# A 14-unit wait in the order planner of a four-layer gated cross-attention kernel: group 1 joins the last attention later

## The chip, the core and the metric

The kernel runs on one core of a Trainium2 chip. The metric is device time in microseconds (us) of one execution; lower is better. A core has one matmul engine (TensorE, PE in the profile; its weight loads are listed as PEld), a vector engine (DVE), an activation engine (ACT), a general-purpose engine (POOL) and an engine that here only issues DMA transfers (SP). Each works through its own instruction list strictly in the order in which the program wrote it; they meet through semaphores.

## What is computed

The input is `x` of 4 batches of 256 tokens with 128 features, and a context of the same size. Four layers follow one another; each adds a gated cross-attention and then a gated feed-forward to `x`. What matters here is the end of layer 2 and layer 3:

```python
x = x + tanh(g_xattn[2]) * L2_xattn(layernorm(x), ctx, ctx)      # 16 heads of 8
x = x + tanh(g_ffn[2])   * L2_ffn(layernorm(x), ...)             # quantised matrix + LoRA
x = x + tanh(g_xattn[3]) * L3_xattn(layernorm(x), ctx, ...)      # 16 heads of 64
x = x + tanh(g_ffn[3])   * L3_ffn(layernorm(x), ...)             # 8 experts, best 2 per token

def L3_xattn(latents, context, ...):
    q  = layernorm(latents) @ Wq;  k, v = split(layernorm(context) @ Wkv)
    a  = softmax(clip(q k^T / 8, -11, 11))
    return (a v) @ Wo + bo

def L3_ffn(x, ...):
    top2 of softmax(x @ gate_w^T)                  # two experts for each token
    y  = sum over the two of w_e * (silu(x @ gate_e) * (x @ up_e)) @ down_e
    return y + (silu(x @ sh_gate) * (x @ sh_up)) @ sh_down
```

All arithmetic is in 32-bit floats.

## The kernel before

**Groups and streams.** The four batches form two groups of two: group 0 holds batches 0 and 1, group 1 holds batches 2 and 3. `chain(g)` (L1370) takes one group through all layers. The kernel does not leave the order of the instructions to a scheduler: `tc.manual_schedule` (L1395) keeps on all five engines the order in which Python issued them. That order comes from a small planner (L240 to L256). A `Stream` is a Python generator which issues some instructions and then yields a number, its own estimate of how long they take. `run_streams` always advances the stream whose planned time `at` is lowest, and adds the yielded number to it. So a yielded number is a position in the plan and no instruction: nothing in the finished program waits for it. Group 1 starts `LATER` = 28 units behind group 0, and the second batch of a group `BETWEEN` = 16 units behind its first.

**Layer 2 and the join.** `attention8` (L306) computes layer 2's attention for one batch, `finish2` (L1190) its feed-forward. For each batch of the group one such stream is made (`second`, L1389). `attention64` (L569) then runs layer 3's attention of the two batches as one software pipeline, and its `begin(h)` joins the layer-2 stream of a batch before it starts that batch (`start3`, L1227).

**Layer 3's attention.** For each batch there are four steps. The tiles carry names such as `sc_a3_1_2` (layer 3, batch 1, chunk 2); the texts below write `sc_1_2` for short. Per step PE does: `pw_qh`, `pw_kh` (projections, L444), `sc` (two score tiles, L472), `pv` (values, L458), `po` (weighted values, L486), `ps` (row sums, L501). ACT takes the exponential of the scores (L1214) and DVE clips it (L1215). Then `divide` (L517): DVE takes the reciprocal of the row sums (`rs`, L518, 128x256) and, for the second batch of a group, PE spreads it over the rows (`pb`, L526) and DVE multiplies (L533); for the first batch it goes by DMA through memory (L538, L543) to L550. `output` (L553) makes `pf_a` and adds to `x` (L567). `start3` needs two layernorms of `x` and one of the context, each transposed on PE (`pt_lT`, `pt_cT`, L1221).

**Routing and experts.** `prepare3` (L1239) makes for each batch the layernorm `x3f`, its transposition (`pt_f`, L294), the router's logits (`f3lg`, L1248) and their softmax, whose exponential runs on ACT (L644). `route3` (L1288) needs both batches of the group: on DVE it finds the best two experts of each token (`hot_f`, L686), on PE it counts tokens for each expert (`pc_f`, L691), on DVE it computes each token's slot (`si_f`, L725), and POOL scatters the rows (`rows_f`, eight indirect DMAs, L744). Beside it `shared3` (L1257) computes the shared expert (`pp_f3sh`, `sl_f3sh`, `f3hs`, `py_f3s`). `feed3` (L1310) fetches the sorted rows (`xs_f`, L770) and runs 15 blocks of 128 slots. A block takes from DVE a copy of the expert's weights (`st_f`, L808) and of the rows (`xT_f`, L1318), from PE a transposition (`pt_f`, L810), eight matmuls (`pp_f`, L1324) and four of the block before (`py_f`, L819), from ACT the activation (`sl_f`, L1283), and from DVE the product (`h_f`, L1284). The down weights of a block come by DMA (`wd_f`, L801). At the end come a store (L826), eight gathers on POOL (L851), sums on DVE and the store of `x`.

**Buffers and tables.** PSUM gives eight tiles of one bank in turn to all of these. ACT's exponential and its activation of the experts lie in different tables, so a change from one to the other inserts a table load, which some of the lines below show as `ACT_TABLE_LOAD`.

The functions that the diff touches, and what calls them:

Of the kernel before, what the change touches and what calls it, by code (L numbers as in the profile page):

```python
# [21 lines left out]
G = 2  # L22
# [6 lines left out]
FEATS, PAIRS, VALUES = 20, 7, 5  # L29
BLOCK = P  # L30
LATER = 28.0
BETWEEN = 16.0
ROUND = 12582912.0

# [2 lines left out]
def flamingo_kernel(ctx: ExitStack, tc: tile.TileContext, a: dict, out: bass.AP):  # L37
# [52 lines left out]
    def load(name, shape, src, tag=None):  # L90
        t = wts.tile(shape, F32, tag=tag or name, name=name, bufs=1)
        nc.sync.dma_start(out=t, in_=src)
        return t

    def expert_weights(name, width, src):

        t = wts.tile([P, E, 1024], F32, tag="wexp", name=name, bufs=1)
        for e in range(E):
            nc.sync.dma_start(out=t[:, e, 0:width], in_=src[e])
        return t  # L100
# [157 lines left out]
    def joined(*others):  # L258
        while not all(s.done for s in others):
            yield 0.5  # L260
# [308 lines left out]
    def attention64(batches, start, done, after):  # L569

        hs = [Heads64(b) for b in batches]
        begun, ends = {}, []
        for h, before in zip(hs, [None] + hs):
            h.before = before
        steps = [(h, cp) for h in hs for cp in range(4)]

        def at(n):
            return steps[n] if 0 <= n < len(steps) else None  # L580

        def begin(h):
            yield from joined(after[h.b])
            yield from start(h)

        def ended(h):
            yield HOP
            yield from h.divide()
            yield from h.output()
            yield HOP  # L590
            yield from done(h.b)

        for n in range(-2, len(steps)):
            if n == -2 or (n % 4 == 0 and n // 4 + 1 < len(hs)):
                h = hs[0 if n == -2 else n // 4 + 1]
                begun[h] = Stream(begin(h))
            two, one, this = at(n + 2), at(n + 1), at(n)
            if two and two[1] == 0:
                yield from joined(begun[two[0]])
            if one:  # L600
                one[0].scores(2 * one[1])
                yield 0.9
            if two:
                two[0].project(two[1])
                yield 1.7
            if this:
                this[0].values(this[1])
                yield 1.3
                this[0].sums(this[1])
                yield 0.9  # L610
                if this[1] == 3:
                    ends.append(Stream(ended(this[0])))
            if one:
                one[0].scores(2 * one[1] + 1)
                yield 0.9
            if one and one[1] % 2 == 0:
                one[0].project_values(one[1] // 2)
                yield 1.7
            if two and two[1] == 3:
                two[0].projected = True  # L620
        yield from joined(*ends)
# [453 lines left out]
    def route1(g):  # L1075
        fe, ne, scs, again = zip(*(normed1[G * g + i] for i in range(G)))
        sc = small.tile([P, GT, E], F32, tag="lg", name=f"f1s_{g}")
        for i in range(G):
            nc.vector.tensor_copy(sc[:, i * T : (i + 1) * T, :], scs[i])
        m = small.tile([P, GT], F32, tag="smm", name=f"f1m_{g}")  # L1080
        nc.vector.tensor_reduce(m, sc, AX.X, ALU.max)
        hot = yield from first_is_max(sc, m, f"f1_{g}")
        yield 0.5
        r = Routed(g, f"f1_{g}")
        yield from r.assign([hot], lambda t: ne[t // T][0][:, t % T, :], again)

        al = small.tile([P, GT], F32, tag="al", name=f"f1al_{g}")
        nc.scalar.activation(al, m, AF.Sigmoid)
        pw = ps_mm([E, GN], f"f1pw_{g}")
        for t in range(GT):  # L1090
            nc.tensor.matmul(pw[:, t * P : (t + 1) * P], lhsT=hot[:, t, :], rhs=ident, start=True, stop=True)
        hotT = feat(f"f1hT_{g}")[0:E, :]
        evac(hotT, pw)
        yield 1.5
        pb = ps_mm([P, GT, D], f"f1pb_{g}")
        for t in range(GT):
            nc.tensor.matmul(pb[:, t, :], lhsT=hotT[:, t * P : (t + 1) * P], rhs=b2r, start=True, stop=True)
        acc = work.tile([P, GT, D], F32, tag="acc", name=f"f1acc_{g}")
        nc.vector.tensor_copy(acc, pb)
        groups1[g] = (r, fe, al, acc)  # L1100
        r.fetch(0)
        yield 4.0


    def feed1(g):
        r, fe, al, acc = groups1[g]

        def turn(xT, st, pt):
            nc.vector.tensor_scalar(xT, pt, st[:, 516:517], st[:, 517:518], ALU.mult, ALU.add)

        def up(st, xT, name):
            pp = ps_mm([P, 4, P], f"ph_{name}")
            h = feat(f"h_{name}").rearrange("p (f q) -> p f q", f=4)
            for f in range(4):
                nc.tensor.matmul(pp[:, f, :], lhsT=st[:, f * P : (f + 1) * P], rhs=xT, start=True, stop=True)
            for f in range(4):
                bf = st[:, 512 + f : 513 + f]
                if f < 2:
                    nc.scalar.activation(h[:, f, :], pp[:, f, :], AF.Relu, bias=bf)
                else:  # L1120
                    nc.vector.tensor_scalar(h[:, f, :], pp[:, f, :], bf, 0.0, ALU.add, ALU.max)  # L1121
            return h

        yield from r.run(518, shared["we1"], a["L1f_down"], turn, up, 1.9)
        nc.vector.tensor_tensor(acc, acc, r.out[0], ALU.add)

        for t in range(GT):
            ft = fe[t // T][:, t % T, :]
            xt = x[G * g + t // T][:, t % T, :]
            nc.vector.scalar_tensor_tensor(acc[:, t, :], acc[:, t, :], al[:, t : t + 1], ft, ALU.mult, ALU.add)  # L1130
            nc.vector.scalar_tensor_tensor(xt, acc[:, t, :], tg[:, 5:6], xt, ALU.mult, ALU.add)
        yield 1.5
# [222 lines left out]
    def beginning(b):  # L1355
        yield from attention8(b, start0, finish0, 0)
        yield from feed0(b)

    def weights1():
        yield from joined(*begun0.values())  # L1360
        shared["we1"] = expert_weights("we1", 518, a["L1f_experts"])
        late = wts.tile([P, 7, D], F32, tag="small", name="late", bufs=1)
        shared["shg"] = late[:, 0:2, :].rearrange("p c d -> p (c d)")
        shared["shu"] = late[:, 2:4, :].rearrange("p c d -> p (c d)")
        shared["shd"] = late[:, 4:6, :]
        nc.sync.dma_start(out=shared["shg"], in_=a["L3f_sh_gate"])
        nc.sync.dma_start(out=shared["shu"], in_=a["L3f_sh_up"])
        nc.sync.dma_start(out=shared["shd"], in_=a["L3f_sh_down"].rearrange("(c p) d -> p c d", p=P))

    def chain(g):  # L1370

        batches = [G * g + i for i in range(G)]

        first = {b: Stream(beginning(b), BETWEEN * i) for i, b in enumerate(batches)}
        begun0.update(first)
        if g == 1:
            shared["loads"] = Stream(weights1())
        yield from attention64(batches, start1, prepare1, first)
        if g == 1:

            shared["wq"] = load("wq3", [P, 1024], a["L3x_Wq"], tag="xwq")
            shared["wkv"] = load("wkv3", [P, 2048], a["L3x_Wkv"], tag="xwkv")
            shared["wo"] = load("wo3", [P, 8, D], a["L3x_Wo"].rearrange("(c p) d -> p c d", p=P), tag="xwo")
        yield from joined(shared["loads"])
        yield from route1(g)
        yield from feed1(g)
        if g == 1:
            shared["we3"] = expert_weights("we3", 1024, a["L3f_experts"])
        second = {b: Stream(attention8(b, start2, finish2, 2), BETWEEN * i) for i, b in enumerate(batches)}  # L1389
        yield from attention64(batches, start3, prepare3, second)  # L1390
        yield from route3(g)
        yield from feed3(g)

    ET = mybir.EngineType
    with tc.manual_schedule(engines={ET.PE, ET.DVE, ET.Activation, ET.Pool, ET.SP}):  # L1395
        for g in range(B // G):
            Stream(chain(g), LATER * g)
        Stream(small_constants(), 11.0)
        Stream(empty_slots(), 20.0)
        Stream(quantised(), 60.0)  # L1400
        run_streams()
# [105 lines left out]
```

## Time and profile before

| | |
|---|---|
| Median of 3 runs | 806.35 us (805.9 to 808.5) |
| The profiled execution's own time | 805.46 us |
| Its span in the trace | 803.7 us |
| PE busy | 719.7 us, 90% of the span |
| DVE, ACT, POOL busy | 58%, 39%, 17% |
| Mean granted PE clock | 0.958 |
| PE's last matmul ends | 784.6 us into the span |

The profile was taken of one execution, 805.46 us long; 1.8 us of it lie outside the span. "Busy" of PE means that some matmul was in flight. In lines of the timeline the columns are the start, the duration, the engine, the source line, the operation, out<-in, the number of instructions merged into the line, and in brackets how long the engine had been idle before and what ended the idle time. The granted clock is the share of its full clock that the matmul engine was given. Layer 2 of group 1 ends about 540 us into the span, layer 3's attention runs until about 686 us, and the experts from 687 us to the end.

### The profile page before, as it was taken

To read this page: it belongs to the slowest core of one execution; us is meant where nothing else is said; L and a number is where in the kernel's file an instruction comes from. 1 tells how busy PE (TensorE), PEld (TensorE's weight loads), DVE (VectorE), ACT (ScalarE), POOL (GpSimd) and SP (SyncE) were. 2 spreads that over 40 slices of the span, in tenths; PEclk is the share of its full clock that TensorE was granted. 3 is DMA by queue.
4 is the path that set the end of the run, shared out by engine and by line. 5 is a ranking of instruction groups with operands and counts; after the bars stand their busy time and mean duration, and the time that the engine had idled before them with its cause. 6 is when DMAs were issued, how large, how long until landed. Compare 5 with 4: busy or idle time off the path is not lost.

```text
span 803.7 us, 14819 instructions
## 1 busy us (share of the span) xinstructions
PE 719.7 (90%) x5756; PEld 515.6 (64%) x5756; DVE 462.6 (58%) x1179; ACT 314.9 (39%) x609; POOL 133.5 (17%) x233
## 2 busy tenths in 40 slices
PE   5989998999999998997897899979999988799990
PEld 4556676766666665597864456546666645599990
DVE  3475573556577587775767476553454436665461
ACT  2536555343444423232453445435542442322330
POOL 3010121321110001313212131010000004040043
PEclk9899999999999999999997899999999989999995
DMA  6820101101023002354471000000100200435631
GB/s 202 239 61 2 54 2 53 54 1 54 1 76 110 2 8 53 97 199 150 135 261 39 1 28 2 1 1 1 53 8 1 60 1 24 148 89 146 164 106 49
DMA packets 52986, 54.98 MB, mean 68 GB/s; under 512 B 7274, under 2 KB 40084, under 8 KB 52660
## 3 DMA queue, kind: packets, MB, share of 16 engines
q1 hardware_dynamic: 41252, 44.07, 18.5%
q10 hardware_dynamic: 10128, 6.82, 2.8%
q0 software_dynamic: 1536, 3.15, 1.3%
q8 instruction: 45, 0.74, 0.4%
q14 instruction: 25, 0.20, 0.1%
HBM read 44.52 MB, written 9.50 MB: 67 GB/s over the span
## 4 chain that ended last, share of the span: by engine, by line
PE 70%; DVE 15%; issue 6%; ACT 4%; POOL 2%; DMA 2%; DVEq 0%; POOLq 0%; ACTq 0%; SPq 0%
PE po_a L486 7%; PE sc_a L472 7%; PE pp_f L1324 6%; DVE nmx L338 4%; PE py_f L819 4%; PE po_a L374 4%; PE ps_a L501 4%; PE sc_a L328 4%; PE pf_a L559 3%; PE st_a L355 3%; PE pw_qh_a L444 3%; PE pv_a L458 3%; PE pw_kh_a L444 3%; PE f0pp L987 2%; PE pb_a L526 2%
## 5 line engine op out<-in xcount | busy, mean ns | idle before, releaser
L338 DVE TENSOR_REDUCE nmx<-sc_a 128x2 f32<-128x512 f32 x128 | 79.4, 683 | 27.1 <-PE sc_a L328 27.1
L366 ACT ACTIVATE pw_a<-st_a 128x512 f32<-128x512 f32 x128 | 66.1, 605 | 36.7 <-PE st_a L355 36.6
L472 PE MATMUL sc_a<-qh_a,kh_a 64*128 64x256 f32 x512 | 69.8, 402 | 0.6 <-DVE kh_a L72 0.4
L1042 ACT ACTIVATE pr_a<-pr_a 128x1024 f32<-128x1024 f32 x32 | 33.8, 1057 | 91.7 <-DVE pr_a L1041 85.4
L486 PE MATMUL po_a<-pr_a,va_a 128*64 128x256 f32 x512 | 63.3, 392 | 1.1 <-ACT va_a L76 0.6
L472 PEld LDWEIGHTS sc_a<-qh_a,kh_a 64*128 64x128 f32 x512 | 46.5, 190 | 23.1 <-issue 10.3
L1324 PE MATMUL pp_f<-xT_f,st_f 128*128 128x128 f32 x480 | 58.7, 276 | 1.9 <-DVE xT_f L1318 1.9
L819 PE MATMUL py_f<-wd_f,h_f 128*128 128x128 f32 x416 | 56.7, 279 | 1.7 <-DVE h_f L1121 1.7
L1324 PEld LDWEIGHTS pp_f<-xT_f,st_f 128*128 128x128 f32 x480 | 56.1, 192 | 3.3 <-issue 2.6
L819 PEld LDWEIGHTS py_f<-wd_f,h_f 128*128 128x128 f32 x416 | 51.8, 195 | 2.8 <-DVE h_f L1121 2.1
L486 PEld LDWEIGHTS po_a<-pr_a,va_a 128*64 128x64 f32 x512 | 35.2, 139 | 24.4 <-issue 5.6
L1215 DVE TENSOR_SCALAR pr_a<-pr_a 128x1024 f32<-128x1024 f32 x32 | 22.1, 691 | 47.7 <-ACT pr_a L1214 47.7
L1038 DVE SCALAR_TENSOR_TENSOR pr_a<-maskT,sc_a 128x512 f32<-128x512 uint8 x64 | 40.9, 680 | 11.7 <-PE sc_a L472 11.6
L1214 ACT ACTIVATE pr_a<-sc_a 128x512 f32<-128x512 f32 x64 | 34.0, 604 | 33.0 <-PE sc_a L472 33.0
L328 PE MATMUL sc_a<-kp,qp 32*128 32x256 f32 x512 | 44.2, 429 | 0.3 <-DVE lT L1223 0.3
L355 PE MATMUL st_a<-qm_a,kp 32*128 32x256 f32 x512 | 40.8, 428 | 2.4 <-DVE qm_a L348 2.4
L374 PE MATMUL po_a<-pw_a,va_a 128*32 128x256 f32 x512 | 42.5, 412 | 0.0
L494 ACT COPY oT_a<-po_a 128x512 f32<-128x512 f32 x32 | 18.6, 586 | 50.2 <-PE po_a L486 48.7
L355 PEld LDWEIGHTS st_a<-qm_a,kp 32*128 32x128 f32 x512 | 26.0, 200 | 17.7 <-DVE nmx L338 7.0
L1284 DVE TENSOR_TENSOR h_f<-pp_f,sl_f 128x512 f32<-128x512 f32 x30 | 20.6, 688 | 25.4 <-PE pp_f L1324 15.9
L851 POOL DMA_INDIRECT yg_f<-back_f,si_f x24 | 23.9, 994 | 67.8 <-DMA back_f<-ys_f 42.0
L991 POOL TENSOR_TENSOR wide<-f0wb,wide 128x512 f32<-128x512 f32 x16 | 20.3, 1270 | 88.9 <-DVE wide L990 80.4
(337 smaller groups left out, 1329.6 us busy)
## 6 DMA issues: line engine op xcount, KB each, us to landing
wd_f<-in_L3f_down_dram SPq DMA_DIRECT2D x30, 256.0 KB, 3.2
wd_f<-in_L1f_down_dram SPq DMA_DIRECT2D x22, 256.0 KB, 4.0
f0wb<-f0wd SPq DMA_DIRECT2D x32, 128.0 KB, 3.2
rb_a<-rw_a SPq DMA_DIRECT2D x16, 256.0 KB, 3.8
we<-in_L3f_experts_dram SPq DMA_DIRECT2D x8, 512.0 KB, 9.1
xs_f<-rows_f SPq DMA_DIRECT2D x10, 256.0 KB, 3.6
back_f<-ys_f ACTq DMA_DIRECT2D x10, 256.0 KB, 5.7
we<-in_L1f_experts_dram SPq DMA_DIRECT2D x8, 259.0 KB, 5.4
```

The source lines that it names most:

```text
L328: nc.tensor.matmul(self.sc[j][:, qt, :], lhsT=self.qp[c // 2][r, c % 2, qt * P : (qt + 1) * P], rhs=self.kp[c // 2][r, c % 2, :], start=Tr ...
L338: nc.vector.tensor_reduce(self.nmx[c % 2][:, :, j, 8], self.sc[j], AX.X, ALU.max, negate=True)
L355: nc.tensor.matmul(st[j][:, kt, :], lhsT=self.kp[c // 2][r, c % 2, kt * P : (kt + 1) * P], rhs=self.qm[c // 2][r, c % 2, :], start=True, s ...
L366: nc.scalar.activation(pw[:, i], st[2 * n + i], AF.Exp, scale=SCALE8)
L374: nc.tensor.matmul(po[r, :], lhsT=self.va[:, kt, 4 * c + j, :], rhs=pw[j // 2][:, j % 2, kt, :], start=(kt == 0), stop=(kt == T - 1),)
L444: nc.tensor.matmul(pp[:, ci, :], lhsT=w[:, c * P : (c + 1) * P], rhs=src, start=True, stop=True)
L472: nc.tensor.matmul(sc[jj][:, kt * S : (kt + 1) * S], lhsT=self.kh[c // 2][r, c % 2, kt * P : (kt + 1) * P], rhs=self.qh[c // 2][r, c % 2, ...
L486: nc.tensor.matmul(po[64 * jj : 64 * jj + 64, ci, :], lhsT=self.va[cp // 2][:, kt, 4 * (cp % 2) + 2 * ci + jj, :], rhs=self.prs[2 * cp + c ...
L819: nc.tensor.matmul(py, lhsT=h[:, f, :], rhs=wd[:, f * P : (f + 1) * P], start=(f == 0), stop=(f == 3))
L1038: nc.vector.scalar_tensor_tensor(pr[:, jj, :], maskT[:, b].rearrange("p t q -> p (t q)"), -1e32, sc[jj], ALU.mult, ALU.add)
L1214: nc.scalar.activation(pr[:, jj, :], sc[jj], AF.Exp)
L1324: nc.tensor.matmul(pp[i][:, f * P : (f + 1) * P], lhsT=st[:, 512 * i + f * P : 512 * i + (f + 1) * P], rhs=xT, start=True, stop=True,)
```

## The change

A constant `FURTHER` = 14 is added. A new generator `middle(b)` runs layer 2's attention of a batch and, for the batches of group 1 (`b >= G`), yields 14 at its end. `chain` makes its streams `second` from it. Since `attention64` joins these streams, layer 3 of batches 2 and 3 stands 14 units later in the plan than it did. No instruction of the computation, tile or transfer is added or taken away; what changes is the order in which the instructions of the two groups alternate from there on.

```diff
 LATER = 28.0
+FURTHER = 14.0
 BETWEEN = 16.0
...
+    def middle(b):
+        yield from attention8(b, start2, finish2, 2)
+        if b >= G:
+            yield FURTHER
+
...
-        second = {b: Stream(attention8(b, start2, finish2, 2), BETWEEN * i) for i, b in enumerate(batches)}
+        second = {b: Stream(middle(b), BETWEEN * i) for i, b in enumerate(batches)}
         yield from attention64(batches, start3, prepare3, second)
         yield from route3(g)
         yield from feed3(g)
```

The order is settled when the program is built, so it can be read from the program. The engines' lists are the same up to the end of group 1's layer 2. From there on, with all in PE's list and the line numbers of the kernel before:

| | before | changed |
|---|---|---|
| first projections of batch 2 (`pw_2_0`) | straight behind those of batch 1 | behind batch 1's third |
| `pc_f` of group 0 | behind `sc_3_6` of batch 3 | ahead of `sc_3_2` of batch 3 |
| first block of group 0's experts | behind the output of batch 3 | ahead of `ps_3_3`, before batch 3's division |
| batch 3's `pb` and `pf_a` | in one piece | between blocks 0 to 3 of group 0 |
| `pc_f` of group 1 | behind block 2 of group 0 (from 0) | behind block 7 |
| first block of group 1 | behind block 9 of group 0 | behind block 14, the last |

ACT's list grows from 620 to 622 entries: two table loads more.

## The prediction

> **What bounds the kernel now.** I read first the page's head and its slices.
>
> ```profile
> span 803.7 us, 14819 instructions
> PE 719.7 (90%) x5756; PEld 515.6 (64%) x5756; DVE 462.6 (58%) x1179; ACT 314.9 (39%) x609; POOL 133.5 (17%) x233
> ...
> PE   5989998999999998997897899979999988799990
> ...
> PEclk9899999999999999999997899999999989999995
> ```
>
> PE is the full engine, and DVE has room. A slice is 20.1 us: in the changed part (from slice 26, about 525 us) PE dips at the end of layer 2 (slice 26) and in slices 32 to 34, 643 to 703 us, where group 0's routing, batch 3's division and group 1's routing lie. The windows say how deep: busy PE is the third number.
>
> ```profile
> 620.00:640.00 20.00, 20.00 (x152) 13.45 (x148) 8.72 (x20) 7.18 (x14) 0.92 (x2) 1.00 0.24 60
> 640.00:660.00 20.00, 16.14 (x85) 8.40 (x86) 9.77 (x33) 7.60 (x12) 0.00 (x0) 0.85 0.00 1
> 660.00:680.00 20.00, 16.60 (x145) 11.44 (x141) 10.78 (x37) 6.28 (x9) 6.85 (x13) 0.98 0.05 17
> 680.00:700.00 20.00, 16.18 (x121) 13.67 (x121) 11.01 (x41) 6.34 (x9) 4.64 (x8) 1.00 0.47 143
> 740.00:760.00 20.00, 20.00 (x182) 20.00 (x181) 9.02 (x18) 6.21 (x15) 0.00 (x0) 1.00 0.50 140
> ```
>
> Then PE's waits from 540 us on, which name who is late, and PE's timeline, which gives place and price.
>
> ```profile
> PE pc_f L691 <- DVE hot_f L686: 5.1, 2, 3.4
> PE pb_a L526 <- DVE rs_a L518: 4.2, 2, 3.4
> PE pp_f L1324 <- DVE xT_f L1318: 1.9, 2, 1.4
> PE pt_f L810 <- DMA xs_f<-rows_f: 1.7, 1, 1.7
> PE f3lg L1248 <- DVE f3x L72: 1.7, 1, 1.7
> ```
>
> ```profile
> 654.46 1.03 PE L691 MATMUL pc_f<-hot_f,tri 128*128 128x32 f32 x4 [3.42 <-DVE hot_f L686]
> ...
> 657.29 3.60 PE L486 MATMUL po_a<-pr_a,va_a 128*64 128x256 f32 x16
> ...
> 669.85 1.95 PE L486 MATMUL po_a<-pr_a,va_a 128*64 128x256 f32 x16
> ...
> 676.20 1.95 PE L526 MATMUL pb_a<-rs_a,ident 128*64 128x256 f32 x16 [3.40 <-DVE rs_a L518]
> ```
>
> The waits are answers from DVE's in-order list, hardly from its load. And a wait can cost twice: the 16 `po` matmuls behind the 3.42 us gap took 3.60 us, the same 16 later 1.95.
>
> **The account before.** From the first changed place to PE's last matmul (784.6 us) PE waited, in order: 4.4 us at layer 2's end (1.01, 3.20 and 0.18), 0.8 at batch 1's `pb`, 0.4 at its `pt_f`, 3.4 at `pc_f`, 3.4 at batch 3's `pb`, 2.2 at the first block (DMA 1.70, copy 0.47), 1.7 at the last `f3lg`, 1.7 at group 1's `pc_f`, 1.4 at its first block: 19.4 us. Half clock came on top: granted clock 0.50 from 654 to 660 us, by rows 0.4 (`pc_f` 1.03 against 0.63) + 1.0 (shared expert 2.05 against 1.02) + 1.65 (`po`) = 3.1 us; and about 1.5 us at 534 to 537 (one `sc` 1.70 against 1.13, `pz` 1.03 against about 0.5, and the transpositions).
>
> **The change part by part.** The 14 units are no instruction, so the wait itself costs nothing. Matmuls and transfers stay in number, so I carry PE's work over at its rows: `sc` 1.07 us, a pair of projections 1.93, `po` 1.88, `ps` 1.00, `pv` 1.9, half of `pf_a` 2.4, an expert block 2.79. The 19.1 us behind the last matmul (store, gathers, sums) keep their order. What is left is where PE waits in the new lists. I set PE's work between two points against the chain of its partner: exponentials 1.15 us after the scores end, clip 0.69, reciprocal 1.75, `st` copy 0.69, an evacuation 0.6 to 0.7, a small routing operation 0.2, a table load 1.28.
>
> 1. Layer 2's end. The layernorms of batch 2 leave DVE, so `x2f` comes about 1 us earlier; but `pt_lT`, `pt_cT` of batch 2 leave PE too (1.1 us). Waits 4.4 us as before: gain nothing, the work comes later.
> 2. New: `pt_cT` of batch 2 waits for its normalised context, which on DVE now stands behind clip `pr_1_1` and batch 0's reciprocal. From the end of `sc_1_1`: 1.15 + 0.69 + 1.75 + 0.6 = 4.2; PE has `pv` and one `sc`, 3.0. Wait 1.15 us.
> 3. Batch 1's `pb`. From the end of `ps_1_3` PE has `ps_2_1`, `sc_2_5`, `pv`, one transposition: 4.3 us; DVE's reciprocal ends behind clip `pr_2_5` and two statistics after 6.1. Wait 1.75 (was 0.8).
> 4. Batch 1's `pt_f`: `x3f` now stands behind clip `pr_2_7`, whose scores end 1.0 us before PE wants it: 1.15 + 0.69 + 0.6 − 1.07 = 1.3 (was 0.4).
> 5. Group 0's `pc_f`. DVE's list has batch 2's reciprocal in the middle of the chain to `hot_f`: value copy ready 0.9 us before PE comes free, then 0.7 + `f3hs` (its `sl` 0.8 us after PE is free, 0.7) + 1.75 + three small ones 0.6: wait 4.0 (was 3.4). A gap longer than the one that halved the clock: I keep 3.1 us for that.
> 6. `py_f3s` now stands only one pair of projections behind `sc_3_2`, and ACT must do two exponentials, a table load and `sl` first: 1.15 + 1.28 + 0.6 + 0.7 = 3.8 against 1.9. At half clock the projections take 3.8 us and cover it: 0.3; at full clock it would be 1.7. `po_3_1` adds 0.2.
> 7. First block. From `pc_f` PE has 32 us of batch 3's work. Slots to rows: POOL's eight scatters no longer stop for a layernorm (8 x 1.27 us), fetch and landing 4.4 as between 683.13 and 687.57 us. The rows are there 8 us early. The 2.2 us go.
> 8. Batch 3's `pb` now stands behind block 0. DVE has the reciprocal behind `h` of block 0 and the copies of blocks 1 and 2: from the end of `pp` of block 0 0.05 + 0.7 + 0.7 + 0.3 + 1.75 = 3.5, up to 4.1 if `sl` is late behind the table load; PE has one small transposition. Wait 3.8 (was 3.4). Half clock behind it: below.
> 9. Last `f3lg` 0.8 (was 1.7): `py_f` stands ahead of it. Group 1's `pc_f` 2.2 (was 1.7): a weight copy and a table load pair, 2 x 1.28, in the softmax. Group 1's first block 0.7 (was 1.4): two copies instead of three ahead of it. The two new table loads stand there and in block 3, where 4.8 us of `pf_a` cover them; without cover they cost 2.6.
>
> The page "ScalarE: Activation LUTs" of the Trainium skill (What ACT_TABLE_LOAD costs) speaks against the change here: it gives a switch 1283 ns and a drain of 1380 behind it, and by that estimate two more loads would be 5.3 us, and where nothing covers them the sum +8.8. Here the load at 661.54 us took 1.28 and the activation began at 662.83, so this trace shows no drain.
>
> Waits after: 4.4 + 1.15 + 1.75 + 1.3 + 4.0 + 0.3 + 0.2 + 0 + 3.8 + 0.8 + 2.2 + 0.7 = 20.6 us, against 19.4: +1.2 us.
>
> Half clock: the rows show that gaps of 3.2 and 3.42 us were followed by it and one of 3.40 us was not (`pb` at 676.20 us, granted clock 1.00). For item 8's 3.5 to 4.1 us I take it, priced between the two cases, 1.5 and 3.1: 2.3 us. Together +3.5 us. If it is not halved: +1.2.
>
> The page "TensorE: Matmul & The Clock Gate" of the Trainium skill (Part 1) says that the clock falls to half after a free-running idle window of about 3.4 us. Read strictly, whether a gap of 3.4 to 4 us holds a whole window is chance, so by it item 8 would more often cost nothing and the sum be +1.2; the 3.2 us gap here, with half clock behind it, says that less suffices.
>
> **The rivals.** (a) The same waits, but the clock stays full at item 8: +1.2 us, 806.7 for the profiled execution. It has the 3.40 us gap for it, and the other two gaps against it. (b) Faster: group 0's routing is covered by batch 3's attention at `pc_f` as it is at the first block. Place: item 5. If `hot_f` is ready when PE arrives, 4.0 and 3.1 us go, 1.4 of item 6 come back, and without item 8's half clock the sum is 3.5 − 5.7 − 2.3 = −4.5: 801.0, with the shift below 801.9. It decides against the forecast once the wait at `pc_f` is under about 3 us, since then the clock also stays. For it: PE has 8.6 us between `f3lg` and `pc_f` where it had 7.7. Against it: the reciprocal of 1.75 us that now stands inside that chain. Covering all of slices 32 to 34 (15.5 us with the half clock) I exclude, since item 8's wait is written into DVE's list. (c) Far slower: group 1's experts now run alone for 15 blocks instead of 9, and one stream cannot fill PE. Against it: alone a block took 2.79 us at 761 to 784 us, side by side the same. 0.3 us a block would be 1.8 us. (d) The change does nothing: excluded, since the engines' lists differ.
>
> **How the numbers follow.** The sum is made against the profiled execution, 805.46 us (span 803.7 and 1.8 around it): 809.0. The median of the runs lies 0.9 above it, so I forecast 809.8. Slower by over 0.3%, about what a measurement of this kernel can tell from no change and here 2.4 us, holds 0.56: the forecast, and (c). Between lies 0.27, rival (a) at 807.6. Faster by over 0.3% holds 0.17, rival (b) at 801.9. The range: below, no half clock at `pc_f` nor at `pb` and item 6 at 1.7 is +1.2 − 3.1 + 1.4 = −0.5, and the 1.5 us at layer 2's end may go too, −2.0: 804.3; I take 804. Above, two half clocks of 3.1 and item 6 at 1.7 is +1.2 + 3.1 + 1.4 = +5.7, with a further gap's 1.5 to 2.5 behind items 2 to 4: 814.5. What lies under 804 is most of (b).
>
> **What would show it.** Right: waits at batch 2's `pt_cT`, batch 1's `pb`, `pc_f` near 4 us and batch 3's `pb` between blocks 0 and 1 near 3.8; no wait for `xs_f`; granted clock 0.5 behind `pc_f` and behind that `pb`; blocks of group 1 alone at 2.79 us. Wrong: `pc_f` without a wait, or a gap that only a larger cause than DVE's order explains.

## The result and the profile after

The changed kernel takes 811.4 us (median of 14 runs, 809.0 to 818.6), the kernel before 806.7 us (14 runs beside them). The ratio is 1.0064, 95% interval 1.0039 to 1.0089: slower by 3 to 7 us. Measured again later, the ratio was 1.0090 (1.0057 to 1.0123). The forecast was 809.8 us in a range of 804 to 814.5.

The head of the page of the changed kernel and two rows of its 40 slices (tenths of a slice that PE is busy, and the granted clock):

```profile
span 809.1 us, 14826 instructions
...
PE 718.8 (89%) x5756; PEld 513.9 (64%) x5756; DVE 461.9 (57%) x1179; ACT 317.6 (39%) x611; POOL 133.6 (17%) x233
...
PE   5889998999999998998896898989989797989990
...
PEclk9999999999999999998997899979999899999996
```

The profiled execution is 810.85 us long, 809.1 of it in the span, against 805.46 and 803.7 before. PE's busy time is the same (718.8 us, before 719.7), so the time was lost between the matmuls. Half clock, which lengthens busy time, took 23.8 us in the whole span before and 21.3 after. Counted from 0, the dips to 8 and 7 of the last attention now lie in slices 29, 31, 33 and 35, where they were in 32 to 34. The windows of the same stretches (busy PE stands after the first comma, the granted clock third from the end):

```profile
620.00:640.00 20.00, 17.08 (x117) 9.62 (x115) 8.84 (x32) 9.04 (x17) 0.92 (x2) 1.00 0.00 0
640.00:660.00 20.00, 14.94 (x91) 10.04 (x92) 8.54 (x30) 8.50 (x13) 3.41 (x7) 0.83 0.27 66
660.00:680.00 20.00, 20.00 (x170) 12.45 (x169) 8.60 (x15) 8.08 (x16) 6.10 (x10) 1.00 0.41 126
680.00:700.00 20.00, 15.79 (x117) 12.19 (x116) 11.68 (x27) 5.26 (x9) 0.94 (x2) 0.91 0.12 31
740.00:760.00 20.00, 19.21 (x171) 18.84 (x171) 10.28 (x21) 6.03 (x14) 5.05 (x8) 1.00 0.68 185
```

From 640 to 660 us PE is busy for 14.9 us (before 16.1). Between 660 and 680 it is full, where it had 16.6. From 680 to 700 it is down again at a clock of 0.91. The same kind of hole has moved and deepened; it was not filled. PE's waits from layer 2's end to its last matmul:

```profile
PE pc_f L692 <- DVE hot_f L687: 6.4, 2, 4.7
PE pb_a L527 <- DVE rs_a L519: 6.3, 2, 4.2
PE pt_x L295 <- DVE x2f L283: 3.8, 1, 3.8
PE py_f3s L1274 <- DVE cum_f L701: 1.7, 1, 1.7
PE pt_f L295 <- DVE x3f L283: 1.6, 1, 1.6
```

`pc_f` waits 4.70 us for group 0 and 1.66 for group 1, `pb` 4.21 for batch 3 and 2.10 for batch 1, `py_f3s` 1.66 where it waited for nothing. The timeline of PE, DVE and ACT around `pc_f` of group 0 shows what stands ahead of what:

```profile
637.68 1.02 PE L1265 MATMUL pp_f3sh<-f3x,late 128*128 128x512 f32 x2
...
637.88 0.58 ACT L77 COPY va_a<-pv_a 128x512 f32<-128x512 f32 x1 [1.69 <-PE pv_a L459]
638.49 1.28 ACT L1284 ACT_TABLE_LOAD   x1
639.78 0.60 ACT L1284 ACTIVATE sl_f3sh<-pp_f3sh 128x512 f32<-128x512 f32 x1
...
640.41 0.69 DVE L1285 TENSOR_TENSOR f3hs<-pp_f3sh,sl_f3sh 128x512 f32<-128x512 f32 x1 [2.35 <-ACT sl_f3sh L1284]
641.02 1.74 DVE L519 RECIPROCAL rs_a<-rs_a 128x256 f32<-128x256 f32 x1
...
643.40 1.03 PE L692 MATMUL pc_f<-hot_f,tri 128*128 128x32 f32 x4 [4.70 <-DVE hot_f L687]
...
646.23 2.08 PE L473 MATMUL sc_a<-qh_a,kh_a 64*128 64x256 f32 x8
...
652.11 1.38 PE L1274 MATMUL py_f3s<-late,f3hs 128*128 128x128 f32 x10 [1.66 <-DVE cum_f L701]
```

PE has no work from 638.70 us on. ACT first copies values (637.88), then loads a table, then computes `sl` (until 640.38); DVE makes `f3hs`, then batch 2's reciprocal of 1.74 us, and only then the last steps to `hot_f`. After the gap the clock is half: `pc_f` takes 1.03 us instead of 0.63 at full clock and `sc` 2.08 instead of 1.13. The same two engines around batch 3's `pb`:

```profile
684.22 1.74 DVE L519 RECIPROCAL rs_a<-rs_a 128x256 f32<-128x256 f32 x1
...
686.02 1.98 PE L527 MATMUL pb_a<-rs_a,ident 128*64 128x256 f32 x8 [4.21 <-DVE rs_a L519]
```

I account for the stretch from the start of layer 2's last output (`pfo`) to PE's last matmul in three terms: PE's waits, the time lost to half clock (busy time times one minus the granted clock, in windows of 1 us), and the rest, which is work at full clock. Before: 256.8 us = 19.4 + 4.7 + 232.6. After: 267.0 = 22.8 + 10.7 + 233.5. The tail behind PE's last matmul is 19.1 and 19.0 us. The work at full clock is 0.9 us more. The waits are 3.4 us longer, and half clock took 6.0 us more in these two executions. Ahead of the stretch, where both kernels have the same instruction lists, half clock took 19.1 us in one and 10.6 in the other. So its amount in a single profile is largely chance, and the experiments had to tell what of it belongs to the change.

### The profile page after: what moved, and what is told of

It reads as the page before. It is cut to its first block, busy times and chain, and to the rows that moved or that the text cites. A ratio compares the mean times of both kernels' runs of the same rounds, so it can differ in the third digit from the quotient of the medians.

```text
span 809.1 us, 14826 instructions
## 1 busy us (share of the span) xinstructions
PE 718.8 (89%) x5756; PEld 513.9 (64%) x5756; DVE 461.9 (57%) x1179; ACT 317.6 (39%) x611; POOL 133.6 (17%) x233
## 3 DMA queue, kind: packets, MB, share of 16 engines
q1 hardware_dynamic: 41252, 44.07, 18.1%
## 5 line engine op out<-in xcount | busy, mean ns | idle before, releaser
L1039 DVE SCALAR_TENSOR_TENSOR pr_a<-maskT,sc_a 128x512 f32<-128x512 uint8 x64 | 40.9, 681 | 11.7 <-PE sc_a L473 11.6
L502 PE MATMUL ps_a<-pr_a,pick 128*32 128x256 f32 x512 | 33.8, 384 | 0.0
```

The costliest lines, as they stand in the source:

```text
L502: nc.tensor.matmul(ps[32 * k : 32 * k + 32, :], lhsT=pick[:, cp, :], rhs=pr[k // 2][:, k % 2, kt * S : (kt + 1) * S], start=(kt == 0), sto ...
L1039: nc.vector.scalar_tensor_tensor(pr[:, jj, :], maskT[:, b].rearrange("p t q -> p (t q)"), -1e32, sc[jj], ALU.mult, ALU.add)
```

## Experiments

Three theories. **A**: the change costs what the new in-order lists make PE wait, above all for DVE's 128x256 reciprocal, and the half clock behind gaps that are already long. **B**: the distance between the groups costs by itself, because one group's work cannot fill PE. **C**, a rival on the clock alone: half clock comes and goes with something else than these gaps.

**Reciprocals earlier.** The edit lets `divide`'s reciprocal be issued right behind the last addition to the row sums, instead of later, behind other work on DVE:

```diff
+EARLY = ("a3_3",)                    # which batches
 # where the row sums are added up
+                if cp == 3 and self.name in EARLY:
+                    nc.vector.reciprocal(self.rs, self.rs)
 # in divide
-            nc.vector.reciprocal(self.rs, self.rs)
+            if self.name not in EARLY:
+                nc.vector.reciprocal(self.rs, self.rs)
```

Batch 3 alone, in the changed kernel:

> The changed kernel, with one instruction moved: batch 3's reciprocal of the row sums in layer 3 is issued directly behind its last addition, ahead of the copies and the product of the first expert blocks. Theory A (a wait is DVE's order, and the clock halves behind a long wait): the wait at batch 3's division goes from 4.2 us to under 0.7 us, the half clock behind it (1.6 us in the profile of the change) goes too; 4 to 6 us less than the changed kernel, about 806 us. Theory B (the distance between the groups costs by itself, because one group alone cannot fill PE): the wait comes back at the next matmuls that need DVE, block 1 of the experts; total within 1 us of the changed kernel.

Measured: 805.7 us, ratio 0.9977 (0.9945 to 1.0010). The wait at `pb` of batch 3 fell from 4.21 to 0.18 us and all others stayed within 0.2 us:

```profile
678.81 1.08 PE L531 MATMUL pb_a<-rs_a,ident 128*64 128x256 f32 x8 [0.18 <-DVE rs_a L513]
```

One instruction of DVE in another place takes back the whole loss. This does not say that the loss stood at that place: the wait there was 3.40 us before the change, so the change added only 0.8 to it. The edit saves a wait that both kernels have.

Batch 2 alone:

> The changed kernel, with batch 2's reciprocal in layer 3 issued directly behind its last addition, so that it no longer stands between the two halves of the search for the best two experts. Theory A: the wait at the expert count of group 0 goes from 4.7 us to about 3.0 us (1.7 us of reciprocal leave the end of the chain, but stand before the softmax instead, where the chain has slack until the values' copy), and half clock behind it is as likely as before or rarer: 1.5 to 4 us less than the changed kernel, 808 to 810 us. Theory B: within 1 us of the changed kernel.

Measured: 813.4 us, ratio 1.0064 (1.0036 to 1.0092). `pc_f` of group 0 waited 3.09 us instead of 4.70 and `py_f3s` 0.83 instead of 1.66, and the time did not follow. The gap of 3.09 us was still followed by half clock (3.2 us lost there), so the edit could save only its 2.3 us of waits, about as much as the interval leaves open. Its runs had no less half clock than those of the kernel before (last column of the table below). A miss for the time, a hit for the wait.

All four batches, in the changed kernel (`EARLY` with all names) and in the kernel before:

> The changed kernel, with all four reciprocals of layer 3 issued directly behind the last addition. Theory A: besides the two moves of the other runs the wait at batch 2's context transposition (0.9 us) and the one at batch 1's division (2.1 us, and its half clock of 1.7 us) go: 8 to 13 us less than the changed kernel, 799 to 803 us, so faster than the kernel before. Theory B: at most 2 us less.

> The kernel before, with all four reciprocals of layer 3 issued directly behind the last addition. Theory A: the wait at batch 3's division goes from 3.4 us to about 2.3 us, the one at batch 1's division (0.8 us) goes, the ones at the expert counts stay; 1 to 4 us less than the kernel before, 803 to 806 us. If theory A holds, the greater distance is then no loss of itself, and the changed kernel with early reciprocals is the faster of the two by 2 us or more, since there the wait for the sorted rows is hidden. Theory B: the kernel before with early reciprocals stays 3 us or more ahead of the changed one with them.

Measured: 804.2 us, ratio 0.9956 (0.9928 to 0.9983) for the changed kernel, 810.5 us, ratio 0.9991 (0.9955 to 1.0028) for the kernel before; theory A had expected less for both (799 to 803 and 803 to 806 us). PE's waits of the changed kernel with all reciprocals early:

```profile
PE pc_f L696 <- DVE hot_f L691: 4.8, 2, 3.1
...
PE pb_a L531 <- DVE rs_a L513: 0.2, 1, 0.2
```

and of the kernel before with the same edit:

```profile
PE pt_f L814 <- DMA xs_f<-rows_f: 4.1, 2, 3.7
...
PE pb_a L530 <- DVE rs_a L512: 2.4, 1, 2.4
```

In the first, `pb` waits 0.2 us in all and the sum of the waits is 15.9. In the second, `pb` still waits 2.4, and the sorted rows come no earlier, so that PE waits 3.7 for them instead of 1.7: the sum is 20.0, no gain. With this edit the kernel with the larger distance has the shorter time: the intervals of the two ratios overlap, but the medians of 12 runs each, taken in the same series, lie 6.3 us apart. Theory B expected the kernel before to stay 3 us or more ahead; it falls for a distance of 14.

**Distance.** Half of it, twice it, and only the second batch later:

```diff
-FURTHER = 14.0
+FURTHER = 7.0        # and 28.0 in another kernel
```

```diff
-        if b >= G:
+        if b > G:            # FURTHER stays 14
```

> The change with 7 units instead of 14. Theory B: half of the loss, about 809 us. Theory A: the loss follows the places of the reciprocals and not the distance; with 7 units batch 3's division stands again before block 0, so the 4.2 us there go back to about 3.4 or less; waits of 18 to 22 us, 805 to 810 us.

> One part of the change alone: only batch 3 gets the 14 units. Batch 2 alternates with batch 1 as before. Group 0's expert count stands behind fewer matmuls of batch 3, and group 0's first block comes behind batch 3's division again. Theory A: waits between those of the two kernels, 19 to 23 us in sum from layer 2's end on; the wait for the sorted rows stays, the one of batch 2's context transposition does not appear; 806 to 810 us. Theory B (distance): half of the loss, 809 us, whatever the waits.

> The distance doubled (28 units instead of 14), nothing else. Theory B (distance itself costs): more than at 14 units, 816 us or above, about +10 us against the kernel before. Theory A (the wait goes by which instruction stands behind which): no order by distance, since 7 units already cost more than 14; the time should follow the sum of TensorE's waits in its own list by the line that the eight kernels so far give, about 1.5 us of time for each us of wait beyond the 19.4 us of the kernel before (19.4 gives +0, 22.8 gives +5, 25.4 gives +10). If the waits come out near 20 us and the time above 814 us, theory A falls.

Measured: 817.9 us at 7 units (ratio 1.0134, 1.0096 to 1.0171), 811.5 us with only batch 3 later (1.0055, 1.0020 to 1.0091), 831.5 us at 28 units (1.0326, 1.0290 to 1.0362). The expectations of 805 to 810 us at 7 units and of 806 to 810 with only batch 3 later were misses: I had no working for the new lists and took a point between. Waits at 7 units:

```profile
PE pc_f L692 <- DVE hot_f L687: 6.1, 2, 4.3
PE pt_x L295 <- DVE x2f L283: 4.4, 1, 4.4
...
PE pt_f L811 <- DMA xs_f<-rows_f: 2.4, 1, 2.4
PE po_a L487 <- DVE va_a L73: 2.1, 1, 2.1
```

The smaller distance waits 25.4 us, more than the larger one: layer 2's end 4.4, group 0's `pc_f` 4.3, batch 3's `pb` 3.3, a value copy on DVE 2.1, rows by DMA 2.4. At 28 units the sum is 37.5, and one wait makes it:

```profile
PE pt_f L811 <- DMA xs_f<-rows_f: 21.7, 1, 21.7
```

There group 0's last block ends at 745.0 us and group 1's rows are not sorted yet. POOL's list has group 0's eight gathers (748.7 to 758.4 us) ahead of group 1's last three scatters, of which this is the first:

```profile
758.73 1.00 POOL L745 DMA_INDIRECT rows_f<-x3f,si_f  x1 [0.30 <-issue]
```

PE goes on with the fetched rows at 766.7. The other waits sum to 15.7 us, fewer than in any other kernel without fill. The time alone also fits theory B, which expected 816 us or above; the waits say that the partner's work had run out altogether, and that some 10 of the 21.7 us are again the order of one engine's list, POOL's. Below 28 units the sum of the waits goes up and down with no order by distance: 19.4 us at none, 25.4 at 7, 22.8 at 14.

**Filling the gaps.** Idle matmuls of 128x256, each of which the trace shows as two entries and about 0.46 us, put in front of the instruction that waits, into a tile that it overwrites (the edit shortened):

```diff
+FILL = (6, 3, 7, 6)      # pt_x of batch 3, pb of batch 1, pc_f of group 0, pb of batch 3
+    def warm(dst, n):
+        for _ in range(n):
+            nc.tensor.matmul(dst, lhsT=ident, rhs=tri, start=True, stop=True)
```

> The changed kernel, with idle matmuls (128x256, into tiles that the next matmuls overwrite) ahead of four waits: 6 before batch 3's transposition at layer 2's end, 3 before batch 1's division, 7 before group 0's expert count, 6 before batch 3's division. They fit inside the waits of 3.8, 2.1, 4.7 and 4.2 us at 0.48 us each, so no matmul of the computation starts later for them. Theory A with the clock as its second half: the half-clock stretches behind these four places (5.0, 1.7, 2.4 and 1.6 us lost in the profile of the change) mostly go; 4 to 10 us less than the changed kernel, 801 to 807 us. Rival C (the half clock is set by something other than these gaps, or does not matter for the end): within 1.5 us of the changed kernel, or slower where a filler runs at half clock.

> The changed kernel with all four reciprocals early, and 6 idle matmuls before batch 3's transposition at layer 2's end and 4 before group 0's expert count. Theory A: the waits stay as with the early reciprocals alone (15.9 us), and the half clock behind the two remaining long gaps goes: 2 to 6 us less than that run's 804 us. Rival C: no less than it.

> The kernel before (without the 14 units) with idle matmuls of about 2.8 us each in its three gaps of 3.2 to 3.4 us (batch 3's layer-2 input, group 0's routing, batch 3's division). Theory A: the waits shrink by what the matmuls take, so the waiting itself ends as before, and only half clock behind two of the gaps (4.7 us in its profile) can go: 2 to 4 us less than the kernel before, 802 to 805 us. Theory C (half clock is set by something else): no change or slower by up to 1 us, with half clock still there in its profile.

Measured: 809.1 us, ratio 1.0021 (0.9991 to 1.0050) for the changed kernel with fill `(6, 3, 7, 6)`; 802.1 us, 0.9930 (0.9903 to 0.9958) with early reciprocals and fill `(6, 0, 4, 0)`; 800.1 us, 0.9917 (0.9883 to 0.9950) for the kernel before with fill `(6, 0, 6, 6)`. The last is the plainest, since nothing but the matmuls differs. PE at group 0's routing in it:

```profile
646.27 2.86 PE L69 MATMUL pc_f<-tri,ident 128*128 128x256 f32 x12
649.67 0.63 PE L703 MATMUL pc_f<-hot_f,tri 128*128 128x32 f32 x4 [0.55 <-DVE hot_f L695]
```

and three windows of it behind the three filled gaps (granted clock third from the end):

```profile
528.00:536.00 8.00, 7.30 (x37) 4.76 (x36) 5.77 (x22) 1.82 (x4) 3.00 (x7) 1.00 0.00 0
648.00:656.00 8.00, 7.45 (x58) 4.98 (x60) 2.30 (x5) 3.57 (x6) 0.00 (x0) 1.00 0.00 0
668.00:676.00 8.00, 7.65 (x59) 5.23 (x59) 4.41 (x13) 1.78 (x3) 6.43 (x12) 1.00 0.13 45
```

The matmuls take 2.86 us of the gap of 3.42 and leave a wait of 0.55, so `hot_f` is no earlier; but the clock stays at 1.00 in all three places. Its waits (11.0) and fill (18 x 0.46 = 8.3) are 19.3 us together, as before (19.4), and its half clock in the stretch is 1.7 us. The gain of 0.83%, 6.7 us, is more than the 2 to 4 us expected, and half clock is what is left to explain it. The granted clocks of all runs agree: their mean is 0.967 over the 12 filled runs and 0.957 over the 17 of the kernel before beside them. In the changed kernel waits (14.7) and fill (10.1) make 24.8 us against 22.8. Only 0.4 of the difference lies at the four filled places; 1.5 lies at group 1's first block, whose rows come by DMA, and why they came later is not shown. The time was 0.4% less than the changed kernel's all the same, with intervals that overlap; 4 to 10 us had been expected. The two fastest kernels, at 0.9917 and 0.9930, beat both kernels of this case and are not told apart by their intervals.

**A second profile of both kernels**, unaltered:

> The changed kernel unaltered, profiled a second time, to see what of its account is chance. Theory A: waits within 0.3 us of the first profile's at each place, sum near 22.8; half clock again behind the gaps of 3.8 to 4.7 us, but with another sum than 10.7 us, likelier smaller, since the medians leave about 1.8 us for half clock beyond that of the kernel before. Theory C: half clock at other places than behind these gaps.

> The kernel before unaltered, profiled a second time. Theory A: waits within 0.3 us of the first profile's, sum near 19.4 (the one for rows brought by DMA may differ by 1 us); half clock behind some of the gaps of 3.2 to 3.4 us, 1.5 to 6 us in the changed stretch, and another sum ahead of the stretch than the 19.1 us of the first profile.

Measured: for the changed kernel waits of 22.9 us (first 22.8), each place that was 0.5 us or longer within 0.3; half clock 9.8. For the kernel before waits of 19.0 (19.4), half clock 14.6, where the first profile had 4.7 and 1.5 to 6 were expected; this execution took 817.2 us, one of the longest of that kernel on record, so its length is used for nothing. What matters in it is one line:

```profile
682.40 2.58 PE L526 MATMUL pb_a<-rs_a,ident 128*64 128x256 f32 x16 [3.40 <-DVE rs_a L518]
```

It is the same gap of 3.40 us that the prediction read as "not followed by half clock". Here the 16 matmuls behind it took 2.58 us instead of 1.95.

All profiles together (change of time: ratio minus one; waits and half clock in the stretch, from single profiles, us). The last column is an estimate from all runs: a run's span times one minus its mean granted clock is the time that half clock took in it, the stretches in which PE idles included. The column gives the mean of this over a kernel's runs, less that of the runs of the kernel before in the same series, with a standard error of 1.2 to 2.0 us.

| Kernel | time | waits | half clock | half clock of all runs, against before |
|---|---|---|---|---|
| changed, all reciprocals early | −0.44% | 15.9 | 9.9 | −3.3 |
| changed, batch 3's reciprocal early | −0.23% | 19.0 | 5.6 | −5.1 |
| before, all reciprocals early | −0.09% | 20.0 | 6.6 | +0.5 |
| before (two profiles) | 0 | 19.4, 19.0 | 4.7, 14.6 | 0 |
| changed, batch 2's reciprocal early | +0.64% | 20.5 | 10.8 | +1.5 |
| only batch 3 later | +0.55% | 21.9 | 13.1 | +1.3 |
| changed (two profiles) | +0.64%, +0.90% | 22.8, 22.9 | 10.7, 9.8 | first series not on record, second −0.5 |
| 7 units | +1.34% | 25.4 | 15.2 | +5.3 |
| 28 units | +3.26% | 37.5 | 14.0 | +11.8, some 9 of it in the long wait |
| before, filled | −0.83% | 11.0 + 8.3 fill | 1.7 | −8.3 |
| changed, early and filled | −0.70% | 11.6 + 4.6 fill | 3.4 | −5.0 |
| changed, filled | +0.21% | 14.7 + 10.1 fill | 1.7 | −6.4 |

Over the kernels without fill a straight line through these points gives 1.44 us of time for each us of wait, with deviations up to 2.8 us, about as much as the intervals allow. For the 37.5 us of waits that the 28-unit kernel turned out to have, the line on record before it ran gives +27 us (1.5 x 18.1); it came at +26. This is an observation over ten points, mostly of one cause; it is no law. That the slope is above 1 fits the half clock only in part: by the last column half clock adds to the loss at 7 units, but not in the changed kernel. Gaps do bring half clock: in the eleven profiles without fill, 31 of 32 gaps of 3.0 us or more were followed by half clock, at 1.6 to 6.8 us each; of nine gaps of 2.0 to 2.4 us, six. Shorter ones I did not count, since most lie close to a longer one. Theory C falls for the long gaps: the three profiles with fill lost 1.7, 3.4 and 1.7 us, the eleven without it 4.7 to 15.2, and the runs with fill have 5.0 to 8.3 us less of it than those of the kernel before.

## Why the prediction was right, and where its steps were not

The sign and the first cause hold: slower, by new waits for DVE's in-order list, +3.5 us forecast, +5.2 (3 to 7) and +7.3 (5 to 10) measured. The second cause, more half clock, is there in one pair of profiles but not in the runs as a whole. The two terms were sized wrongly, in opposite directions, so that the sum came near is in part luck.

| Step | forecast | measured | before |
|---|---|---|---|
| 1 layer 2's end | 4.4 | 4.31 | 4.39 |
| 2 batch 2's `pt_cT` | 1.15 | 0.90 | 0 |
| 3 batch 1's `pb` | 1.75 | 2.10 | 0.83 |
| 4 batch 1's `pt_f` | 1.3 | 1.63 | 0.44 |
| 5 group 0's `pc_f` | 4.0 | 4.70 | 3.42 |
| 6 `py_f3s`, `po_3_1` | 0.3 + 0.2 | 1.66 + 0 | 0 |
| 7 group 0's first block | 0 | 0 | 2.17 |
| 8 batch 3's `pb` | 3.8 | 4.21 | 3.40 |
| 9 last `f3lg`, `pc_f`, first block | 0.8 + 2.2 + 0.7 | 0.86 + 1.66 + 0.79 | 1.66 + 1.72 + 1.41 |
| Sum | 20.6 | 22.8 | 19.4 |

Every wait forecast at over 0.2 us is there, and none of over 0.5 us at a place that was not named. The waits grew by 3.4 us and not by 1.2 (by 3.9 between the second profiles).

- **Step 6 was mis-sized most**, 0.3 for 1.66. The chain was right (exponentials, table load, `sl`, `f3hs`), but half clock was to cover it by stretching the projections to 3.8 us. It fell on `pc_f`, `pp_f3sh` and `sc` instead (643.4 to 648.3 us) and was over; the projections ran at full clock, and the 1.7 that the step gave for that case came out. I spent the same half clock as a cost in one term and as a cover in another, and neither its place nor its length was known.
- **Step 5**, 4.0 for 4.70: the term "`sl` 0.8 us after PE is free" took 1.7, from 638.70 to 640.38. ACT's list has a value copy of 0.58 us ahead of the table load, which I had not put in.
- **Step 8**, 3.8 for 4.21: `sl` of block 0 is late behind its table load, the "up to 4.1" of that step, and I took 3.8, the middle. The experiment with batch 3's reciprocal shows the cause: with the reciprocal early, 4.03 of the 4.21 us go.
- **Steps 3 and 4** were 0.3 too short each, step 9's `pc_f` 0.5 too long: the wait is as before, so the weight copy and the load pair that I added there cost nothing.
- **Half clock**, +2.3. Two single profiles say +6.0, two others −4.8, so profiles do not size it. The runs do better. By the measure of the last column half clock took 33.7 us a run over the changed kernel's 14 runs and 34.0 over its later 6; over the 35, 29 and 17 runs of the kernel before that stand beside the experiments it took 36.3, 34.1 and 34.4. Idle stretches hold 8.2 and 9.7 us of it in the changed kernel's two profiles, 10.1 and 10.6 in those of the kernel before. So the estimate for the term is about 0, with an uncertainty of some 2 us, and the +2.3 is not shown. The place was right: 1.57 and 1.56 us were lost behind batch 3's `pb` in the two profiles. But the mean over the runs is no higher for it.
- **A term put at nothing.** "I carry PE's work over at its rows" took the work at full clock as unchanged. The profiles have 233.5 and 233.7 us of it after, 232.6 and 231.7 before: 0.9 to 2.0 us more. With 3.4 to 3.9 us of waits this makes 4.3 to 5.9 of the loss, so that the loss needs no more half clock. The added work is spread over many matmuls, with 0.4 us at `sc` and 0.3 each at `po` and at the shared expert's `pp_f3sh` as the largest parts; why they take longer in the new order is open.

**The rivals.** (a), the clock stays full behind `pb`: it did not, in either profile. The evidence that I gave (a) was a gap of 3.40 us with full clock behind it, one profile of a thing that changes from run to run; the second profile had half clock behind the same gap. That the clock comes back behind `pb` does not make its price of 2.3 right, see above. (b), routing covered: `pc_f` waits longer, not shorter; the reciprocal within the chain and ACT's list decide, as argued against it. The limit that (b) names, full clock under a wait of about 3 us, does not hold here: six of nine gaps of 2.0 to 2.4 us were followed by half clock. (c), one stream cannot fill PE: the blocks of group 1 alone start every 2.79 us after as before, at 14 units. All 30 blocks' transpositions and matmuls together take 0.3 to 0.5 us more at full clock than before, so (c) has at most that share at 14 units.

The rule that I weighed on ScalarE's table loads ("ScalarE: Activation LUTs", What ACT_TABLE_LOAD costs), a drain of 1380 ns behind the load, is not seen in the changed kernel either: the load at 638.49 us takes 1.28 and `sl` starts at 639.78. The rule of "TensorE: Matmul & The Clock Gate" (Part 1: The HAM clock gate), an idle window of about 3.4 us whose place is chance, is too lenient for this kernel: gaps of 3.0 to 3.43 us were followed by half clock 15 times of 16. The window's chance place fits the other half of what was seen, that the loss varies from run to run.

## What to carry to other kernels

When two streams share in-order engines, the distance between them need not have a price of its own; here it had none up to 14 units. Write down, for each place where the partner's work will be missing, what stands ahead of the awaited instruction on every engine of the chain, the third engine's copies too, and then look for the one long instruction that can move. Here a reciprocal of 1.74 us issued where its input was ready took back as much as 14 units of distance had cost. Do not let a cost whose place is chance cover another cost, and take the price of half clock from the granted clocks of many runs, never from one profile.

## What was not expected of the hardware

- Filling three gaps of 3.2 to 3.4 us with matmuls whose results are thrown away made the kernel before 0.83% faster (0.5 to 1.2), though no awaited result came earlier. Half clock behind those gaps therefore costs it about 6.7 us on average; its two profiles show 4.7 and 14.6, and the clocks of all runs 8.3, idle stretches included.
- Half clock comes mostly in pieces of 1.6 to 1.7 us lost, or two to four of them in a row: behind layer 2's gap of 3.2 us one profile lost 1.64, another 6.74. What decides how many follow was not found.
- The same matmuls take 0.9 to 2.0 us more at full clock in the changed order, and 235.5 us in the 28-unit kernel, the most of the kernels without fill. I did not find why.
